# Smaller first pieces of x and of the weights, and nine warm-up matmuls fewer, in a fused conditional FFN kernel

## The chip, the cores and the metric

The kernel runs on one core of a Trainium2 chip. The metric is the device time of one execution in microseconds (us), from runs on the chip. A core has five engines that work side by side: TensorE (matmul; the profile calls it PE, and its weight loads PEld), VectorE (DVE), ScalarE (ACT), GpSimd (POOL) and SyncE (SP, which here only issues DMAs). DMAs are issued from a queue of SP, of ACT or of POOL, and all share 16 DMA engines.

## The reference

All data are float32; there are 64 x 64 tokens of 1024 features, and each batch entry has one of 16 conditions.

```python
W = weights[condition]                              # (64, 64, 64)
y = jnp.einsum('bct,bcd->bdt', x, W)                # mixes the 64 rows of one batch entry
gate_logits = jnp.einsum('bsd,ed->bse', y, gate_w)  # 8 experts
w, selected = jax.lax.top_k(gate_logits, 2)
w = jax.nn.softmax(w, axis=2)
result = jnp.einsum('bsd,od->bso', y, base_w) + base_b
w_full = sum of one_hot(selected) * w
low = jnp.einsum('bsd,erd->ebsr', y, lora_A)        # rank 16
result = result + 2.0 * jnp.einsum('ebsr,eor,bse->bso', low, lora_B, w_full)
out = x + result
```

## The kernel before, in words

The 4096 tokens are 32 tiles of 128. The condition's product mixes tokens and the other products mix features, so the kernel takes the features first: z = x times one wide matrix made of lora_A, gate_w and base_w (1160 columns, padded and cut into three column blocks of 388, of which the first uses 384), and then mixes the rows of z with a block-diagonal matrix of the tile's conditions, which GpSimd gathers. Top-2 gate, softmax and the LoRA product follow for each tile, and the sum with x and the bias is stored.

Each float32 product is made of three TensorE matmuls: an operand is split into a rounded part (xh, wh: a cast, `copy`, L234) and a remainder (xl, wl: a subtraction on VectorE, `sub`, L231), and the matmuls are wh by xh, wl by xh, wh by xl (`zstep`, L407 to L417, recorded at L414). Features come in four chunks of 256 (k), each of two halves of 128 (f). A weight block is called b*kn* or w*kn*: chunk k (1 to 4), column block n (1 to 3). The first four tiles are multiplied plainly (list PLAIN, L539): for tiles 1 and 2 the order is chunk by chunk, in it column blocks 1 and 2, in them tile 1 and then 2, so the first matmuls are those of w11 with tile 1, w11 with tile 2, w12 with tile 1, w12 with tile 2, then w21 and so on. Column block 3 follows when all chunks are there. From the fifth tile on, pairs of tiles go through a scheme with fewer products of summed operands; sums of weight blocks are prepared early on VectorE (`mix_w`, L338).

Loads at the start: `load_x` (L274) brings one chunk of one tile, 128 KB, on SP's queue; `load_w` (L313) brings a block of 388 KB on SP's queue, but w11 and w12 come as two halves (f) of 194 KB, those of w11 on ScalarE's queue. `split_x` (L280) and `split_w` (L328) cast and subtract; in the first chunk VectorE casts x and w is split half by half.

NWARM = 39 matmuls of a zero tile (L224, L225) run on TensorE before the first data are there. ScalarE loads its activation table in the same time (L324).

The order on each engine is not written by hand: `Program.add` (L88) records every step with engine, estimated cost, buffers read and written, and a due time; `Program.run` (L111) plays a list schedule with these costs and emits the instructions engine by engine. A step depends on the last writer of a buffer's key, so a smaller key lets a step start on part of a tile. Eight semaphores serve the DMAs of the SP and ACT queues in turn, so that such a DMA waits for the landing of the one that stood eight places before it.

Of the kernel before, what the change touches and what calls it, by code (L numbers as in the profile page):

```python
# [20 lines left out]
P = 128  # L21
# [10 lines left out]
W = 388  # L32
N0 = NG + T - 2 * W
CN = (N0, W, W)
OUTS = ((NG, N0, 0), (0, W, N0 - NG), (0, W, N0 - NG + W))
KQ = 4
NPAIR = NT // 2
NPLAIN = 2
TOP = 3.0e38
NWARM = 39  # L40

PE, ACT, DVE, POOL, SP = "PE", "ACT", "DVE", "POOL", "SP"

# [36 lines left out]
class Program:  # L80
# [7 lines left out]
    def add(self, engine, cost, fn, reads=(), writes=(), due=None, first=False, size=0.0, early=None, port=False,  # L88
            after=0.0):

        n = len(self.steps)
        engine, cost = (e if isinstance(e, (list, tuple)) else [e] for e in (engine, cost))
        deps = set()
        for b in list(reads) + list(writes):
            if b in self.writer:
                deps.add(self.writer[b])
        for b in writes:
            deps.update(self.readers.get(b, ()))  # L100
        for b in reads:
            self.readers.setdefault(b, []).append(n)
        for b in writes:
            self.writer[b], self.readers[b] = n, []
        deps.discard(n)
        self.steps.append(dict(eng=dict(zip(engine, cost)), fn=fn, deps=deps, first=first, size=size, port=port,
                               lag=FLIGHT + QUEUE + size * DMA if size else 0.0, after=after,
                               due=self.horizon if due is None else due,
                               early=SP in engine and not reads if early is None else early))
# [59 lines left out]
def cond_ffn_kernel(ctx, tc, xT, x, idx, cw, wall, bias, lb, out):  # L169
# [103 lines left out]

    def load_x(i, k, u):  # L274

        add(SP, ISSUE, lambda e: nc.sync.dma_start(
            xr[:, u].rearrange("p (k n) -> p k n", k=2), xT[i][:, 2 * k:2 * k + 2]), writes=[("xr", u)],
            size=8.0 * P * P)

    def split_x(us, hi=ACT):  # L280

        n = len(us)
        js = xas.two() if n == 2 else [xas.one()]
        add(hi, 0.1 + (0.115 if hi == ACT else 0.09) * 2 * n, lambda e: copy(e, some(xh, js), some(xr, us)),
            [("xr", u) for u in us], [("xh", j) for j in js])
        add(DVE, tt_cost(2 * P * n), lambda e: sub(e, some(xl, js), some(xr, us), some(xh, js)),
            [("xr", u) for u in us] + [("xh", j) for j in js], [("xl", j) for j in js], port=True)
        return js

    def sum_x(os, xs, ys, f):  # L290

        add(DVE, tt_cost(2 * P * len(os)), lambda e: nc.vector.tensor_tensor(some(xr, os), some(xr, xs), some(xr, ys), f),  # L292
            [("xr", u) for u in set(xs + ys) - set(os)], [("xr", u) for u in os], port=True)


    class Block:


        def __init__(self, name, dt=F32):
            self.name, self.dt, self.slot, self.t = name, dt, slots.one(), None  # L300
            self.keys = [("w", self.slot, f) for f in range(2)]

        def ap(self):
            if self.t is None:
# [8 lines left out]
    def load_w(m):  # L313
# [3 lines left out]
        if k == 0 and n < 2:  # L317

            for f in range(2):
                q, dma = (SP, nc.sync.dma_start) if n else (ACT, nc.scalar.dma_start)  # L320
                add(q, ISSUE, lambda e, f=f, dma=dma: dma(b.ap()[:, f:f + 1], wall[k][n][:, f:f + 1]),
                    writes=b.keys[f:f + 1], size=4.0 * P * W, early=False)
            if not n:
                add(ACT, 1.5, lambda e: nc.scalar.activation(warm, warm, AF.Exp))  # L324
            return
# [2 lines left out]
    def split_w(m, p, step=2):  # L328

        b, h, l = raw[m], Block(f"wh_{m}_{p}", F32R), Block(f"wl_{m}_{p}", F32R)  # L330
        hi[p], lo[p] = h, l
        for j in range(0, 2, step):
            a = slice(j, j + step)
            add(ACT, 0.2 + 0.00083 * W * step, lambda e, a=a: copy(e, h.ap()[:, a], b.ap()[:, a]), b.keys[a], h.keys[a])
# [69 lines left out]
    def mm_cost(n):  # L404
        return max(COL * n + SET, LEAST)

    def zstep(key, b, j, p, f, start, stop, cols=W):  # L407


        z, n = bank[b][:, :cols], slice(f * P, (f + 1) * P)  # L410

        def do(e):
            for q, (l, w) in enumerate(((xh, h), (xh, g), (xl, h))):
                nc.tensor.matmul(z, l[:, j, n], w.ap()[:, f, :cols], start=(start and q == 0), stop=(stop and q == 2),  # L414
                                 skip_group_check=True)
        h, g = hi[p], lo[p]
        add(PE, 3 * mm_cost(cols), do, [("xh", j), ("xl", j), h.keys[f], g.keys[f]], [b, "order"], due=due[key])  # L417

    def split_z(n, src, key):

# [1 line left out]
        h, l = zh[q][:, :n], zl[q][:, :n]  # L422
        add(ACT, 0.2 + 0.00085 * n, lambda e: copy(e, h, src()), [key], [("zh", q)])
        add(DVE, 0.09 + 0.00104 * n, lambda e: sub(e, l, src(), h), [key, ("zh", q)], [("zl", q)],
            port=isinstance(key, tuple))
        return q

    def outs(c):
# [152 lines left out]

    for k in range(KQ):
        for i in range(2):
            load_split_x(i, k, hi=DVE if k == 0 else ACT)
            load_split_w(f"b{k + 1}{i + 1}", step=1 if k == 0 else 2)

    chan = sb.tile([P, 1], F32, name="chan")
# [24 lines left out]
    def plain(i, c, k):  # L612
# [8 lines left out]
            if c == 0 and i > 1:  # L621
                load_cond(i)
        ks, m = LASTK if c == 2 and i < 2 else range(KQ), f"b{k + 1}{c + 1}"
        for f in range(2):
            zstep(("plain", i, c, k, f), zb[i, c], xa0[i, k], SINGLE.get(m, m), f, k == ks[0] and f == 0,
                  k == ks[-1] and f == 1, CN[c])
        left[i, k] -= 1
        if not left[i, k]:
            xas.give(xa0[i, k])
# [234 lines left out]
```

## Time and profile before

| | |
|---|---|
| median of 3 runs | 460.17 us (460.08 to 460.25) |
| the profiled execution's own time | 460.46 us |
| its span, first to last instruction | 458.7 us |
| first warm-up matmul | 1.06 us |
| first matmul on data (L414) | 5.02 us |
| first matmul with w12 | 8.10 us |
| first matmul with w21 | 10.23 us |
| DMA in the first 11.5 us / the next 11.5 us | 279 / 352 GB/s |

The page gives busy time, and the chain of work that ended last, followed back from the last instruction. The timeline lists instructions by start; in brackets stands how long the engine was idle before one, and what ended that. Busy matmuls overlap: one of 384 columns takes 0.34 us from start to end, and the next starts 0.175 us after it. SP issued the first loads at these times:

| issue, us | load | landed after, us |
|---|---|---|
| 0.74 | x, tile 1, chunk 1 (SP) | 3.4 |
| 0.74 | w11, f = 0 (ScalarE's queue) | 3.6 |
| 1.18 | x, tile 2, chunk 1 (SP) | 3.8 |
| 1.18 | w11, f = 1 (ScalarE's queue) | 4.1 |
| 1.65, 2.12 | w12, f = 0 and 1 (SP) | 4.2, 4.3 |
| 2.60 | w21 (SP) | 5.5 |
| 3.07 | x, tile 1, chunk 2 (SP) | 5.4 |
| 4.40 | w22 (SP) | 5.0 |

### The profile page before, as it was taken

How to read it: one execution, taken by the hardware profiler on the slowest of the kernel's cores; microseconds unless marked ns; L12 is line 12 of the kernel's file. 1: busy time of each engine (PE TensorE's matmuls, PEld its weight loads, DVE VectorE, ACT ScalarE, POOL GpSimd, SP SyncE). 2: the span in 40 equal slices, each digit the busy share in tenths (PEclk: the TensorE clock that was granted, in tenths of full speed). 3: DMA queues.
4: the chain of work that ended last, by engine and by line, in shares of the span. 5: the costliest groups of instructions: out<-in, count | busy, mean ns of one | idle time of the engine just before them, and what ended most of it. 6: DMA issues, size and time to landing. Idle time of an engine off the chain costs nothing.

```text
span 458.7 us, 7577 instructions
## 1 busy us (share of the span) xinstructions
PE 452.7 (99%) x2621; PEld 449.7 (98%) x2621; DVE 383.5 (84%) x941; ACT 227.2 (50%) x520; POOL 89.6 (20%) x107
## 2 busy tenths in 40 slices
PE   8999999999999999999999999999999999999995
PEld 8999999999999999999999999999999999999995
DVE  5999997879989788796987979789797988888674
ACT  5864666543736345373543646354454544546331
POOL 3030214121303021220303003030210403103000
PEclk9999999999999999999999999999999999999999
DMA  8932748977768462764847456565565746556142
GB/s 279 352 117 47 153 107 198 213 211 202 180 206 202 172 161 87 217 131 163 199 127 202 108 182 148 172 162 133 191 123 185 173 129 193 116 174 149 51 134 91
DMA packets 36229, 75.00 MB, mean 164 GB/s; under 512 B 4432, under 2 KB 22240, under 8 KB 36192
## 3 DMA queue, kind: packets, MB, share of 16 engines
q0 software_dynamic: 10560, 36.72, 33.5%
q1 hardware_dynamic: 25200, 37.32, 25.9%
q10 hardware_dynamic: 432, 0.49, 0.4%
q8 instruction: 20, 0.33, 0.3%
q14 instruction: 17, 0.14, 0.1%
HBM read 57.74 MB, written 16.78 MB: 162 GB/s over the span
## 4 chain that ended last, share of the span: by engine, by line
PE 97%; DMA 1%; DVE 1%; ACT 0%; issue 0%
PE ps_z L414 76%; PE ps_o L447 15%; PE ps_a L447 6%; DMA w_b<-in_w 1%; PE ps_a L500 1%; DVE wl_b_b L231 0%; DVE xtok L457 0%; DVE st L740 0%; ACT wh_b_b L234 0%; DVE xl L231 0%; PE ps_z L447 0%; DVE xh L234 0%
## 5 line engine op out<-in xcount | busy, mean ns | idle before, releaser
L231 DVE TENSOR_TENSOR xl<-xr,xh 128x512 fp32r<-128x512 f32 (+1 forms) x138 | 92.1, 670 | 20.0 <-ACT xh L234 19.8
L414 PE MATMUL ps_z<-wh_t_p,xh 128*128 128x388 f32 (+1 forms) x308 | 105.3, 342 | 0.1
L414 PE MATMUL ps_z<-wh_t_p,xl 128*128 128x388 f32 (+1 forms) x308 | 104.3, 339 | 0.0
L414 PE MATMUL ps_z<-wl_t_p,xh 128*128 128x388 f32 (+1 forms) x308 | 104.3, 339 | 0.0
L234 ACT CAST xh<-xr 128x512 fp32r<-128x512 f32 (+1 forms) x136 | 82.5, 610 | 37.2 <-PE ps_z L414 32.5
L740 DVE TENSOR_TENSOR st<-ps_z,st 128x388 f32<-128x388 f32 x126 | 70.2, 558 | 21.2 <-PE ps_z L414 20.2
L292 DVE TENSOR_TENSOR xr<-xr 128x256 f32<-128x256 f32 (+1 forms) x139 | 69.6, 526 | 3.6 <-DMA xr<-in_xT 3.4
L414 PE MATMUL ps_z<-wh_b_p,xh 128*128 128x388 f32 (+1 forms) x180 | 61.4, 341 | 0.0
L414 PE MATMUL ps_z<-wh_b_p,xl 128*128 128x388 f32 (+1 forms) x180 | 60.9, 338 | 0.0
L414 PE MATMUL ps_z<-wl_b_p,xh 128*128 128x388 f32 (+1 forms) x180 | 60.8, 338 | 0.0
L414 PEld LDWEIGHTS ps_z<-wh_t_p,xh 128*128 128x128 f32 x308 | 57.8, 188 | 1.2 <-DVE st L740 0.7
L414 PEld LDWEIGHTS ps_z<-wl_t_p,xh 128*128 128x128 f32 x308 | 57.9, 188 | 0.0
L414 PEld LDWEIGHTS ps_z<-wh_t_p,xl 128*128 128x128 f32 x308 | 57.9, 188 | 0.0
L464 POOL DMA_DIRECT2D out<-xtok x30 | 16.8, 560 | 193.6 <-DVE xtok L457 89.6
L234 ACT CAST zh<-st 128x388 fp32r<-128x388 f32 (+1 forms) x70 | 36.1, 517 | 22.1 <-DVE st L740 15.2
L381 POOL DMA_DIRECT2D xtok<-in_bias x28 | 27.0, 964 | 96.9 <-DMA xtok<-in_x 89.6
L394 POOL DMA_INDIRECT bdr<-in_cw,rows x32 | 36.9, 1155 | 26.4 <-DVE zl L231 17.7
L457 DVE TENSOR_TENSOR xtok<-ps_o,xtok 128x388 f32<-128x388 f32 (+1 forms) x56 | 30.9, 554 | 11.2 <-PE ps_o L447 10.7
L723 ACT ACTIVATE ps_z<-ps_z 128x388 f32<-128x388 f32 x42 | 20.1, 478 | 40.5 <-PE ps_z L414 39.4
L231 DVE TENSOR_TENSOR zl<-st,zh 128x388 fp32r<-128x388 f32 (+1 forms) x70 | 38.7, 554 | 0.9 <-ACT zh L234 0.6
L414 PEld LDWEIGHTS ps_z<-wh_b_p,xh 128*128 128x128 f32 x180 | 33.8, 188 | 0.2
L414 PEld LDWEIGHTS ps_z<-wl_b_p,xh 128*128 128x128 f32 x180 | 33.8, 188 | 0.0
(143 smaller groups left out, 873.0 us busy)
## 6 DMA issues: line engine op xcount, KB each, us to landing
xr<-in_xT SPq DMA_DIRECT2D x128, 128.0 KB, 3.2
xtok<-in_bias POOLq DMA_DIRECT2D x32, 512.0 KB, 7.1
out<-xtok POOLq DMA_DIRECT2D x30, 512.0 KB, 3.2
xtok<-in_x SPq DMA_DIRECT2D x28, 512.0 KB, 3.6
w_b<-in_w SPq DMA_DIRECT2D x10, 388.0 KB, 5.9
xtok<-in_x POOLq DMA_DIRECT2D x4, 512.0 KB, 6.6
out<-xtok SPq DMA_DIRECT2D x3, 194.0 KB, 2.2
bdr<-in_cw,rows POOLq DMA_INDIRECT x32, 5.3
```

The lines of the kernel that those rows point to most:

```text
L231: eng[e].tensor_tensor(o, a, b.bitcast(F32), ALU.subtract)
L234: (nc.scalar.copy if e == ACT else nc.vector.tensor_copy)(o, a)
L292: add(DVE, tt_cost(2 * P * len(os)), lambda e: nc.vector.tensor_tensor(some(xr, os), some(xr, xs), some(xr, ys), f), [("xr", u) for u in s ...
L381: add(POOL, 1.1, lambda e: nc.gpsimd.dma_start(xtok[j], bias.broadcast_to([P, T]), accum_op=ALU.add), writes=keys, size=TWICE * 4.0 * T * P)
L394: add(POOL, 1.04, lambda e: nc.gpsimd.indirect_dma_start(out=bdr[j], out_offset=None, in_=cw, in_offset=bass.IndirectOffsetOnAxis(ap=rows[ ...
L414: nc.tensor.matmul(z, l[:, j, n], w.ap()[:, f, :cols], start=(start and q == 0), stop=(stop and q == 2), skip_group_check=True)
L447: nc.tensor.matmul(d, l, r, start=(start and m == 0), stop=(stop and m == len(mms) - 1), skip_group_check=True)
L457: add(DVE, 0.09 + 0.00104 * (s.stop - s.start), lambda e: nc.vector.tensor_tensor(xtok[j][:, o], bank[b][:, s], xtok[j][:, o], ALU.add), [ ...
L464: add(POOL, 1.0, lambda e: nc.gpsimd.dma_start(out[i * P:(i + 1) * P, o], xtok[j][:, o]), src, size=4.0 * P * (o.stop - o.start))
L500: add(PE, 0.107, lambda e: nc.tensor.matmul(tp, low[i % 2][:, :ER], ident, is_transpose=True, start=False, stop=False, skip_group_check=True),
L723: add(ACT, 0.2 + 0.00085 * W, lambda e: nc.scalar.mul(z[b], z[x], scale), [BANKS[x]], [BANKS[b]])
L740: add(DVE, 0.09 + 0.00104 * W, lambda e: nc.vector.tensor_tensor(unit(u), a(), b(), f), reads, [ukey(u)])
```

## The change

- The first chunk of tile 1 is loaded as two DMAs of 64 KB, one for each half f, both with a due time that puts them first on SP's queue, and VectorE casts and subtracts each half by itself.
- The half f = 0 of w11 is loaded as two DMAs of 194 columns on ScalarE's queue, and cast and subtracted by columns; the half f = 1 is now one DMA on SP's queue, behind x.
- The first matmuls, of w11's f = 0 with tile 1, run as two sets of three with 194 columns instead of one with 384 (the last four columns are padding).
- NWARM goes from 39 to 30.
- Keys of x and of the weights become finer, so that the halves can be waited for one by one; w keys may be nested lists, which `add` flattens.

```diff
+HALVES = (slice(0, 194), slice(194, W))
...
-NWARM = 39
+NWARM = 30
...
+        reads, writes = ([k for q in ks for k in (q if isinstance(q, list) else [q])] for ks in (reads, writes))
...
     def load_x(i, k, u):
-        add(SP, ISSUE, lambda e: nc.sync.dma_start(
-            xr[:, u].rearrange("p (k n) -> p k n", k=2), xT[i][:, 2 * k:2 * k + 2]), writes=[("xr", u)],
-            size=8.0 * P * P)
+        for a, n in ((0, 1), (1, 1)) if (i, k) == (0, 0) else ((0, 2),):
+            add(SP, ISSUE, lambda e, a=a, n=n: nc.sync.dma_start(
+                xr[:, u, a * P:(a + n) * P].rearrange("p (k n) -> p k n", k=n),
+                xT[i][:, 2 * k + a:2 * k + a + n]), writes=xkeys("xr", [u])[a:a + n], size=4.0 * n * P * P,
+                due=a - 100.0 if n == 1 else None)
+
+    def xkeys(t, us):
+        return [(t, u, f) for u in us for f in range(2)]
...
-    def split_x(us, hi=ACT):
+    def split_x(us, hi=ACT, parts=False):
...
+        if parts:
+            for f in range(2):
+                c, k, x, y, z = slice(f * P, (f + 1) * P), 0.1 + 0.09, ("xr", us[0], f), ("xh", js[0], f), ("xl", js[0], f)
+                add(hi, k, lambda e, c=c: copy(e, xh[:, js[0], c], xr[:, us[0], c]), [x], [y])
+                add(DVE, tt_cost(P), lambda e, c=c: sub(e, xl[:, js[0], c], xr[:, us[0], c], xh[:, js[0], c]),
+                    [x, y], [z], port=True)
+            return js
...
-            self.keys = [("w", self.slot, f) for f in range(2)]
+            self.keys = [[("w", self.slot, f, h) for h in range(2)] for f in range(2)]
...
             for f in range(2):
-                q, dma = (SP, nc.sync.dma_start) if n else (ACT, nc.scalar.dma_start)
-                add(q, ISSUE, lambda e, f=f, dma=dma: dma(b.ap()[:, f:f + 1], wall[k][n][:, f:f + 1]),
-                    writes=b.keys[f:f + 1], size=4.0 * P * W, early=False)
+                q, dma = (SP, nc.sync.dma_start) if n or f else (ACT, nc.scalar.dma_start)
+                for h in range(2) if (n, f) == (0, 0) else (None,):
+                    c = HALVES[h] if h is not None else slice(0, W)
+                    add(q, ISSUE, lambda e, f=f, c=c, dma=dma: dma(b.ap()[:, f, c], wall[k][n][:, f, c]),
+                        writes=[b.keys[f] if h is None else b.keys[f][h]], size=4.0 * P * (c.stop - c.start),
+                        early=False)
...
+        if m == "b11":
+            for f, c, k in ((0, HALVES[0], 0), (0, HALVES[1], 1), (1, slice(0, W), None)):
+                x, y, z = (t.keys[f] if k is None else t.keys[f][k] for t in (b, h, l))
+                n = c.stop - c.start
+                add(ACT, 0.2 + 0.00083 * n, lambda e, f=f, c=c: copy(e, h.ap()[:, f, c], b.ap()[:, f, c]), [x], [y])
+                add(DVE, tt_cost(n), lambda e, f=f, c=c: sub(e, l.ap()[:, f, c], b.ap()[:, f, c], h.ap()[:, f, c]),
+                    [x, y], [z], port=True)
+            return
...
-    def zstep(key, b, j, p, f, start, stop, cols=W):
-        z, n = bank[b][:, :cols], slice(f * P, (f + 1) * P)
+    def zstep(key, b, j, p, f, start, stop, cols=W, half=None):
+        cols = slice(0, cols) if half is None else HALVES[half]
+        z, n = bank[b][:, cols], slice(f * P, (f + 1) * P)
...
-            load_split_x(i, k, hi=DVE if k == 0 else ACT)
+            load_split_x(i, k, hi=DVE if k == 0 else ACT, parts=(i, k) == (0, 0))
...
-        for f in range(2):
-            zstep(("plain", i, c, k, f), zb[i, c], xa0[i, k], SINGLE.get(m, m), f, k == ks[0] and f == 0,
-                  k == ks[-1] and f == 1, CN[c])
+        order = ((0, 0), (0, 1), (1, None)) if (m, i) == ("b11", 0) else ((0, None), (1, None))
+        for n, (f, h) in enumerate(order):
+            zstep(("plain", i, c, k, f), zb[i, c], xa0[i, k], SINGLE.get(m, m), f, k == ks[0] and not n,
+                  k == ks[-1] and f == 1, CN[c], h)
```

## The prediction

> **What bounds the kernel now.** I read the page first, for the engine that carries the end, then the chain that ended last for where that engine did not yet run, then the timeline of the first 16 us and the stretch around 27 us for what it waited for.
>
> ```profile
> span 458.7 us, 7577 instructions
> ...
> PE 452.7 (99%) x2621; PEld 449.7 (98%) x2621; DVE 383.5 (84%) x941; ACT 227.2 (50%) x520; POOL 89.6 (20%) x107
> ...
> PE 97%; DMA 1%; DVE 1%; ACT 0%; issue 0%
> ```
>
> TensorE carries 97% of the chain. A change that leaves its work alone can only win what TensorE idles at the start, or lose there. The chain in order of time (start, length, what) shows that start:
>
> ```profile
> 0.74 3.64 DMA w_b<-in_w
> ...
> 4.40 0.52 ACT wh_b_b L234
> ...
> 6.05 0.49 DVE wl_b_b L231
> ...
> 6.59 19.83 PE ps_z L414 x110
> ```
>
> So the first 6.59 us are: the first piece of w11 lands at 4.38, its cast, its remainder, x's remainder, and from 6.59 matmuls. The timeline (start, length, engine, line, operation, idle before it and what ended it):
>
> ```profile
> 5.00 0.19 PEld L414 LDWEIGHTS ps_z<-wh_b_b,xh 128*128 128x128 f32 x1
> 5.57 0.19 PEld L414 LDWEIGHTS ps_z<-wl_b_b,xh 128*128 128x128 f32 x1 [0.38 <-DVE wl_b_b L231]
> 6.59 0.19 PEld L414 LDWEIGHTS ps_z<-wl_b_b,xh 128*128 128x128 f32 x1 [0.39 <-DVE wl_b_b L231]
> 8.17 0.84 ACT L234 CAST wh_b_b<-w_b 128x776 fp32r<-128x776 f32 x1 [1.25 <-DMA w_b<-in_w]
> 9.04 0.97 DVE L231 TENSOR_TENSOR wl_b_b<-w_b,wh_b_b 128x776 fp32r<-128x776 f32 x1 [1.11 <-ACT wh_b_b L234]
> 11.22 0.42 DVE L231 TENSOR_TENSOR xl<-xr,xh 128x256 fp32r<-128x256 f32 x1
> 11.69 0.19 PEld L414 LDWEIGHTS ps_z<-wh_b_b,xl 128*128 128x128 f32 x1 [0.22 <-DVE xl L231]
> ```
>
> Two things are to be seen. TensorE loses 0.38 + 0.39 us in the first block, as expected. But it waits again at 11.69, for the x remainder of the second chunk's second tile, and that wait is not TensorE's doing: VectorE runs without a gap from 9.04 to the end of that operation (0.97 + 0.42 + 0.97 + 0.42 with small overlaps, 2.60 us), and it starts at 9.04 because w21 landed just before 8.17. **The second stretch hangs on w21's landing, not on when TensorE began.** VectorE then stays busy without a gap until 28.4, where this line stands in front of TensorE:
>
> ```profile
> 25.91 0.95 DVE L231 TENSOR_TENSOR wl_b_b<-w_b,wh_b_b 128x776 fp32r<-128x776 f32 x1
> ```
>
> TensorE's weight load that reads it starts at 26.91, and the matmul after it comes 0.06 us later than the 0.175 us pitch would have it. The cast that this line needs ends at 25.61 (it began at 24.77, after 1.30 us of ScalarE waiting for that block's DMA). So VectorE's line could come at most about 0.3 us sooner unless that DMA comes sooner too. After 27 us no wait over 0.1 us for data stands before 440 us.
>
> **The change part by part.** The program order of the changed kernel as built differs only at the start: the same matmuls, fewer warm-up ones, three more real ones; VectorE three more operations; all queues otherwise in the same order (one 128-column cast of bdr goes one place earlier, into ScalarE time that waits for DMA anyway).
>
> *Warm-up, 39 to 30.* The 39 run from 1.06 to 5.00, 0.101 us each; most have a weight load of 147 ns (the least is 98), so most run on a slow clock and the last few on the full one, with a slow pitch near 0.107. Thirty end at 1.06 + 30 x 0.101 to 0.107 = 4.1 to 4.25.
>
> *First piece of w11, 194 of 388 columns.* The whole piece landed at 4.38. Its half cannot come later; it saves 97 KB at the some 380 GB/s of 3.5 to 5 us, 0.26 us, and, if the x ahead of it shrinks alike, 0.5 us: 3.85 to 4.1, I take 3.95. The cast was 0.51 us at 388 columns and 0.29 at 128: 0.35 at 194, done at 4.3. First real matmul 4.3 instead of 5.02. The remainder (0.56 at 388 columns, 0.27 at 128: 0.34) gives the second at 4.65; the second half follows by about 0.45, its three matmuls done near 5.3.
>
> *Second half of w11 (f = 1), now third on SP's queue instead of second on ScalarE's.* Issue at about 1.65 instead of 1.2, but with only 194 KB of x and halves less in front of it in sum: landing between 4.8 and 5.3 (before: about 5.3), I take 5.05. Cast to 5.56, remainder to 6.1, then its last matmuls and the six of the second tile at 0.175: w12's first matmul at 7.5 to 7.6, where it stood at 8.10. **Gain so far: 0.5 us (0.2 to 0.8).** The six matmuls of 194 columns for three of 384 cost some 0.05 us and lie in the waits.
>
> *VectorE's three more operations.* 2 x 0.27 for 0.42, 2 x 0.34 for 0.56, two casts of 128 columns for one of 0.29: together 0.3 us more, ahead of 9.04. What hides it is the idle 1.11 us before 9.04; without that cover it would be 0.3 us on the path at 11.69.
>
> *SP's queue.* Two more issues at 0.45 us stand before w21, and in the built program every DMA from the ninth on waits for the landing of the one eight before it. w21 was the seventh and went at 2.60 without a wait. Now it is the ninth and waits for the first half of w11: issue at about 4.0. Behind it x21 goes at 4.4 (3.07), w22 at 4.85 (4.40), x22 at 5.3 (4.77); the later ones follow alike, and who waits for them are ScalarE's casts and through them VectorE. Does that delay w21's landing? Issued at 2.60 it landed 5.5 us later, near 8.1, behind 1032 KB. A block of the same size issued at 21.18 landed 3.5 us after its issue. From 4.0 that is 7.5, so the bytes in front decide, not the issue, and they are the same 1032 KB. Before, the stretch 7.0 to 8.0 moved only 264 GB/s where those around it moved 380: a dip of 0.3 us, whose cause the trace does not name. Bounds for w21's landing: 7.5 (no dip) to 8.6 (dip, and a gap in the stream of up to 0.5 because the issue came late). I take 7.95, between the landing of before and that landing without the dip, which is the nearest thing measured.
>
> *Smaller rows.* x11's pieces have 512 bytes per partition, w11's halves 776. The Trainium skill ("DMA: Bandwidth & Descriptors", Specifications) gives 512 B as the least size at line rate; by it these pieces cost nothing. The trace has nothing smaller than 1024 B rows for x to weigh that against; a loss of a fifth on 322 KB would be about 0.15 us at the start and is inside the bounds.
>
> *Sum.* TensorE comes to w21 0.5 us sooner, at 9.7 instead of 10.23. VectorE's run begins 0.15 us sooner. The wait at 11.69 becomes 0.22 + 0.5 - 0.15, about 0.55 us, so 0.35 of the 0.5 goes back, and 0.15 is kept. At 26.91 the same 0.15 shift of VectorE's run lets it stand. The profiled execution took 460.46 us (458.7 of span and 1.8 around it), and would be 460.3; the median of the three runs, 460.17, is 0.29 lower, and I count from that: **460.0 us.**
>
> **The clock, a rule that speaks against it.** Thirty warm-up matmuls are 3.1 us of activity. In the trace the slow weight loads (147 ns, against 98) go on to nearly 5 us, although the granted clock stands at 1.00 in every stretch: its rows do not show this phase. The Trainium skill ("TensorE: Matmul & The Clock Gate", What's actually happening) says that the full clock comes after about 3.4 us of sustained activity, judged in a window that runs freely. By the row, with the change of clock near 4.9 again, nothing is lost: the matmuls of 4.3 to 4.9 wait for data anyway. By the rule, gaps of 0.1 to 0.3 us between 4.1 and 5 may make that window count as idle, and the slow clock then stays for another 3.4 us, to 8.3.
>
> **Rivals.** *The slow clock stays (slower).* Place: from 5.6 to 8.3. Each matmul of 384 columns then costs 0.32 (384/128 of the 0.107 pitch) instead of 0.175: the three of f = 1 end near 6.7, the six of the second tile near 8.6, w12's twelve at 10.7 instead of 10.23, and the matmul of 11.69 comes at 12.1. It decides from the point where the idle between 4.1 and 4.9 is enough for the gate; price 0.4 us, time 460.6. For it: the gaps that my own sum puts there. Against it: TensorE is busy for over four fifths of that stretch. *The stream gaps because w21 waits for the first landing.* w21 lands at 8.6 and VectorE's run starts 0.45 later: 460.6. For it: the issue moves by 1.4 us. Against it: the 3.5 us row. *Supply comes sooner too.* No dip, w21 at 7.5, w22 likewise: VectorE's run moves by 0.6, TensorE keeps its 0.5 and the old wait of 0.22 shrinks: 459.6. For it: the dip is not caused by the change's parts. Against it: the later block at 24.77, which limits the gain to 0.3 unless the whole stream moves. *The gain of the first matmul reaches the end whole:* 459.4, only if everything behind moves alike.
>
> **How the numbers follow.** Main case (w21 about as before, 459.8 to 460.3) 0.45; supply sooner (459.4 to 459.8) 0.22; clock 0.12; stream gap 0.15; both of the last or something unseen, over 461.1, 0.06. The range 459.5 to 460.8 holds the first four but for their edges. A measurement of this kernel tells about 0.2%, 0.92 us, from no change. The first matmul can move by 0.9 us at most (5.0 to 4.1), and only with all of that kept would the kernel be faster by as much, so 0.03; slower by it needs w21 late by 0.9 or the clock slow for two windows, 0.10; the rest, 0.87, within.
>
> **What would show it.** Right: first L414 weight load near 4.3, w12's first near 7.6, ScalarE's cast of w21 starting at 7.7 to 8.3, the wait at 11.69 longer, about 0.5 us, and TensorE unbroken after it. Wrong: a cast of w21 at 8.6 or later (stream gap); matmuls at a pitch of 0.32 beyond 5.5 us (clock); no wait near 11 us (supply sooner). The prediction fails by more than its range only if a later part of the program is moved too, which the order of the built program does not show.

## The result, and the profile after

The changed kernel takes 462.31 us (median of 6 runs, 461.63 to 464.15), the kernel before 460.25 beside it (460.08 to 460.72): 1.0049 times as long, interval 1.003 to 1.0067. It is slower by 2.06 us; the forecast was 460.0, and its range ended at 460.8. The profiled execution took 464.15 us, the longest of the six, with a span of 462.4. The profile therefore shows more of the loss than the median execution had.

First the page: span and instructions, busy time of the engines, and the shares of the chain that ended last.

```profile
span 462.4 us, 7573 instructions
...
PE 455.3 (98%) x2615; PEld 452.9 (98%) x2615; DVE 384.4 (83%) x944; ACT 227.4 (49%) x521; POOL 89.5 (19%) x107
...
PE 97%; DMA 1%; DVE 1%; SPq 0%; issue 0%
```

TensorE still carries 97% of the chain, and its busy time grew by 2.6 us (452.7 before) although it has nine warm-up matmuls fewer. Work that became longer, not only idle time, is what to look for. The chain in order of time (start, length, what) begins with another load than before:

```profile
2.12 4.39 DMA xr<-in_xT
7.55 22.36 PE ps_z L444 x110
```

Before, it began with w11's first piece, and the 110 matmuls began at 6.59. Now it begins with the load of x's tile 2, issued at 2.12 and taking 4.39 us, and they begin at 7.55. The timeline (start, length, engine, line, operation, idle before it and what ended it) had these two operations of VectorE next to each other before the change, the cast of x's tile 2 and the remainder of w11's second half:

```profile
5.76 0.29 DVE L234 CAST xh<-xr 128x256 fp32r<-128x256 f32 x1
5.96 0.57 DVE L231 TENSOR_TENSOR wl_b_b<-w_b,wh_b_b 128x388 fp32r<-128x388 f32 x1
```

After it:

```profile
4.13 0.34 PEld L444 LDWEIGHTS ps_z<-wh_b_b,xh 128*128 128x128 f32 x1
4.68 0.52 ACT L237 CAST wh_b_b<-w_b 128x388 fp32r<-128x388 f32 x1 [0.24 <-DMA w_b<-in_w]
5.42 0.33 PEld L444 LDWEIGHTS ps_z<-wh_b_b,xh 128*128 128x128 f32 x1
6.53 0.29 DVE L237 CAST xh<-xr 128x256 fp32r<-128x256 f32 x1 [1.36 <-DMA xr<-in_xT]
6.94 0.56 DVE L234 TENSOR_TENSOR wl_b_b<-w_b,wh_b_b 128x388 fp32r<-128x388 f32 x1
7.04 0.51 ACT L237 CAST wh_b_b<-w_b 128x388 fp32r<-128x388 f32 x1 [1.84 <-DMA w_b<-in_w]
7.55 0.29 PEld L444 LDWEIGHTS ps_z<-wl_b_b,xh 128*128 128x128 f32 x1 [1.80 <-DVE wl_b_b L234]
7.72 0.33 PEld L444 LDWEIGHTS ps_z<-wh_b_b,xl 128*128 128x128 f32 x1
...
9.17 0.84 ACT L237 CAST wh_b_b<-w_b 128x776 fp32r<-128x776 f32 x1 [0.48 <-DMA w_b<-in_w]
...
13.19 0.33 PEld L444 LDWEIGHTS ps_z<-wl_b_b,xh 128*128 128x128 f32 x1
13.51 0.20 PEld L444 LDWEIGHTS ps_z<-wh_b_b,xl 128*128 128x128 f32 x1
13.88 0.19 PEld L444 LDWEIGHTS ps_z<-wl_b_b,xh 128*128 128x128 f32 x1
```

Four things are to be seen.

- **The start came sooner**, as intended: the first weight load on data at 4.13 instead of 5.00, and w11's second half is cast at 4.68.
- **VectorE is held.** Its cast of x's tile 2 at 6.53 (5.76 before) stands, as before the change, in program order ahead of the remainder of w11's second half, which TensorE needs next. That half was cast by 5.20, but its remainder starts only at 6.94, behind x. TensorE waits 1.80 us for it.
- **TensorE is slow up to 13.51.** From the first one on data, weight loads take about 0.33 us, and from 8.04 they follow each other every 0.32 us; then they take 0.19 us, every 0.175, as they did before from 5.00 on. The granted clock of the windows reads 1.00 in this stretch, because the trace's clock record begins only at 13.52; only the durations tell it here.
- **The other loads are late too**: the first half of w12 is cast at 7.04, w21 at 9.17 (8.17 before). Later profiles show how much w21 varies by itself: 7.1 to 8.3 where the loads come in time.

The windows (columns: stretch, its length, busy time of PE, PEld, DVE, ACT, POOL, granted clock, DMA share, GB/s) of the kernel before and of the changed one show where the loads lost their time:

```profile
4.00:5.00 1.00, 1.00 (x14) 1.00 (x12) 0.34 (x2) 0.51 (x1) 0.00 (x0) 1.00 1.06 377
5.00:6.00 1.00, 0.87 (x7) 0.47 (x4) 1.00 (x4) 0.61 (x2) 0.35 (x1) 1.00 1.07 388
```

```profile
4.00:5.00 1.00, 1.00 (x9) 1.00 (x7) 0.86 (x3) 0.67 (x2) 0.53 (x2) 1.00 1.07 149
5.00:6.00 1.00, 1.00 (x5) 0.75 (x4) 0.17 (x1) 0.20 (x1) 0.75 (x3) 1.00 0.84 213
```

Between 4 and 6 us the changed kernel moves 362 KB where the kernel before moved 765, with the DMA engines shown as nearly as busy (1.07 and 0.84 against 1.06 and 1.07): packets were under way and took longer.

The sum for this execution: the weight load that waited starts at 7.55 instead of 6.59, 0.96 later. From it to the first matmul with w21 is 6.33 us instead of 3.64, 2.69 more: some 18 steps at 0.32 instead of 0.175 are 2.6. Together 3.65 at 13.88. The old wait of 0.22 at 11.69 is gone, so some 3.4 are left at 34 us; then comes a steady drift of about 0.4 until 440 us. The execution took 3.69 us longer.

### The profile page after: what moved, and what is told of

Its sections match the earlier page's. It is cut to its first block, busy times and chain, and to the rows that moved or that the text cites. A ratio compares the mean times of both kernels' runs of the same rounds, so it can differ in the third digit from the quotient of the medians.

```text
span 462.4 us, 7573 instructions
## 1 busy us (share of the span) xinstructions
PE 455.3 (98%) x2615; PEld 452.9 (98%) x2615; DVE 384.4 (83%) x944; ACT 227.4 (49%) x521; POOL 89.5 (19%) x107
## 4 chain that ended last, share of the span: by engine, by line
PE 97%; DMA 1%; DVE 1%; SPq 0%; issue 0%
PE ps_z L444 76%; PE ps_o L479 15%; PE ps_a L479 6%; DMA xr<-in_xT 1%; PE ps_a L532 1%; DVE st L773 0%; SPq L280 0%; DVE xtok L489 0%; DVE wl_b_b L234 0%; DVE zl L234 0%; SPq L340 0%; PE ps_z L479 0%; DVE xl L234 0%; DVE xh L237 0%
## 5 line engine op out<-in xcount | busy, mean ns | idle before, releaser
L234 DVE TENSOR_TENSOR xl<-xr,xh 128x512 fp32r<-128x512 f32 (+2 forms) x139 | 92.4, 667 | 21.5 <-ACT xh L237 21.3
L444 PEld LDWEIGHTS ps_z<-wh_b_p,xl 128*128 128x128 f32 x180 | 33.9, 188 | 0.0
```

Source lines behind the costliest of these rows:

```text
L234: eng[e].tensor_tensor(o, a, b.bitcast(F32), ALU.subtract)
L444: nc.tensor.matmul(z, l[:, j, n], w.ap()[:, f, cols], start=(start and q == 0), stop=(stop and q == 2), skip_group_check=True)
```

## The experiments

Each ran beside the kernel before, whose median was 459.98 to 460.34 us; the ratios are to that. One execution of each was profiled, and times within a kernel are of that execution. In the quoted expectations letters stand for theories: A and B the ones named there, P that the small pieces or short rows stall the loads, Q that w11's second half on SP's queue does, R that x in two loads and the short warm-up each lose by themselves, S that the late issue of w21 stalls the loads, I that the index load does.

### What is it made of

**e1**: the changed kernel again, unchanged.

> The changed kernel once more, unaltered, for a second profile beside the first. The first one shows TensorE idle from 5.9 to 7.55 us, because VectorE's cast of x of tile 2 waits for its DMA until 6.53 and the remainder of w11's second half stands behind it, and matmuls at a pitch of 0.32 us from 7.55 to 13.51 us. If the lost time is that idle and the slow clock after it (theory A), this profile has both again, with 462 us or a little more; the end of the slow pitch may differ, by the stretches of 3.4 us in which the clock is judged. If it was one bad execution of the DMAs (theory B), x of tile 2 lands near 5 us here and the time is near 460.5.

463.06 us, ratio 1.0057 (1.0044 to 1.007). The profile is the same picture: x's tile 2 cast at 6.46, a gap of 1.74 us, weight loads of 0.33 until 13.4. Its six executions took 462.0 to 464.3 us, so the loss isn't a single bad execution.

**e2**: the changed kernel with the old warm-up.

```diff
-NWARM = 30
+NWARM = 39
```

> The changed kernel with 39 warm-up matmuls instead of 30, all else as changed. Theory A1 (the slow clock is the larger part of the loss: 19 matmuls at 0.32 instead of 0.175 make 2.7 us in the first profile): the full clock comes near 5 us, and the time falls to 460.2 to 460.8, although the loads are as late as before. Theory A2 (late loads are the larger part, w21 landing 1.0 us later than before the change): it stays at 461.3 or more, since w21 still lands near 9 us.

461.77 us, 1.0036 (1.0024 to 1.0048), so 1.3 us better than e1 beside it. The loads are as late (x's tile 2 at 6.56), so the gain is the clock's. The profiled execution is one of the longer ones (463.07): with 39 the full clock came before the data did, was kept to the gap, and was lost by it. TensorE idled 2.08 us; then the windows show it:

```profile
6.00:7.00 1.00, 0.00 (x0) 0.00 (x0) 0.44 (x3) 0.00 (x0) 0.72 (x1) 1.00 0.94 320
7.00:8.00 1.00, 0.42 (x1) 0.42 (x2) 1.00 (x4) 0.99 (x2) 0.98 (x1) 0.73 0.99 294
```

TensorE does nothing from 6 to 7, and the granted clock falls to 0.73 in the mean of the next microsecond; weight loads take 0.33 us until 10.6.

**e3**: the kernel before with `NWARM = 30`.

> The kernel before the change with 30 warm-up matmuls instead of 39, all else as before. A1: the gap from 4.2 to 5.0 us and the two waits of 0.4 us in the first block keep the clock slow for at least one more stretch of 3.4 us, to 8 us or later: 460.6 to 462. A2, or warm-up matmuls that matter only by their number: no change, 460.2, since nothing on TensorE was ready before 5.0 us.

460.51 us, 1.0007 (0.9999 to 1.0014), but single executions from 459.82 to 462.19. Its profile has a gap of 0.71 us before 4.88 and full clock after it. In the median nine warm-up matmuls fewer cost little here, but single executions pay; e7 below, whose loads also come in time, pays in the median.

**e4**: the changed kernel with the cast of x's tile 2 on ScalarE, so that VectorE isn't held.

```diff
-            load_split_x(i, k, hi=DVE if k == 0 else ACT, parts=(i, k) == (0, 0))
+            load_split_x(i, k, hi=DVE if (i, k) == (0, 0) else ACT, parts=(i, k) == (0, 0))
```

> The changed kernel with the cast of x of tile 2, first chunk, on ScalarE instead of VectorE, so that the remainder of w11's second half no longer stands behind that load on VectorE. Theory A (the hold on VectorE opens the gap that keeps the clock slow): TensorE goes on with w11's second half near 5.7 us, the gap shrinks to what the load itself leaves, and 0.5 to 1.5 us of the 2.06 come back (460.8 to 461.8). If the late landing alone is the cause: 462 as changed, the wait only moves to tile 2's matmuls.

461.62 us, 1.003 (1.0019 to 1.0041), and the runs lie within 0.67 us of each other (2.5 for the changed kernel). The one gap of 1.80 is now four of 0.16 to 0.61 us, and the clock is full from 4.7 on; it came in this execution before VectorE's hold could matter. The loads are late all the same (x's tile 2 cast at 6.74, w21 at 8.76). So hold and clock together are worth 1.4 us against e1.

### What makes the loads late

**e5** puts w11's second half back on ScalarE's queue in the changed kernel; **e6** puts it on SP's queue, behind x, in the kernel before. The line is e5's, and e6 has its reverse; both also set due times that keep the order of the loads.

```diff
...
-                q, dma = (SP, nc.sync.dma_start) if n or f else (ACT, nc.scalar.dma_start)
+                q, dma = (SP, nc.sync.dma_start) if n else (ACT, nc.scalar.dma_start)
...
```

> The changed kernel with w11's second half back on ScalarE's queue, behind the two 194-column pieces; all pieces and the 30 warm-up matmuls stay. In the profiles so far, the changed loads move 150 to 380 GB/s between 4 and 7 us where the loads of before move 375, x of tile 2 lands at 6.5 instead of 5.0 us and w21 at 8.5 to 9.2 instead of 8.1. Theory Q (the move to one queue does it: only SP's queue carries loads after 4 us, and x of tile 2 stands behind 194 KB more): x of tile 2 lands near 5, w21 near 8.2, and the time is 460.0 to 460.8. Theory P (the small rows, 512 and 776 bytes, do it): x of tile 2 lands after 6, the time stays above 461.5.

> The kernel before with one part of the change: w11's second half on SP's queue, behind x of tile 1, nothing in smaller pieces, 39 warm-up matmuls. Q: x of tile 2 lands after 6 us, w21 near 9, and the time is 461.2 to 462.5. P: x of tile 2 lands at 5.3 or sooner, w21 near 8.2, the time is 460.2 to 460.7.

e5: 461.96 us, 1.0035 (1.0021 to 1.0049); x's tile 2 is cast in time, at 5.38, and w21 at 8.04; now w11's second half is the late one (cast at 5.61, ScalarE having waited 1.32 us for it), and TensorE has a gap of 1.14 us. e6: 461.01 us, 1.0016 (1.0009 to 1.0022), with loads as before (x's tile 2 at 5.70, w21 at 8.33). Q falls as the only cause of late loads: in e6 the queue of w11's second half does not do it alone. It still costs 0.7 us there.

**e7**: the changed kernel with x in one load. **e8**: with w11's first half in one load, x in two. **e9**: as e7, with 39 warm-up matmuls. (Keys and due times that follow from these lines are left out.)

```diff
-        for a, n in ((0, 1), (1, 1)) if (i, k) == (0, 0) else ((0, 2),):
+        for a, n in ((0, 2),):
...
```

```diff
-                for h in range(2) if (n, f) == (0, 0) else (None,):
+                for h in (None,):
...
```

> The changed kernel with the first x load in one DMA of 128 KB again (still first on SP's queue; its cast and remainder stay in halves). P, if the 512-byte rows are what slows the loads: w21 lands near 8.2 and half or more of the 2.06 us comes back (461.2 or less). Q, or the 776-byte rows: as changed, 462 to 463.

> The changed kernel with w11's first half in one DMA of 194 KB again (casts, remainders and matmuls stay in halves of columns; x stays in two pieces). P, if the 776-byte rows slow the loads: w21 lands near 8.2, 461.2 or less. Q, or the 512-byte rows: as changed, 462 to 463; the first matmul comes at about 4.7 instead of 4.2 in either case.

> The changed kernel with x in one load and 39 warm-up matmuls: of the change the w11 pieces, the queue move and the split casts stay. Theory R (two causes, each enough to lose by itself: x in two 512-byte-row loads slows all loads of the first 8 us, as every profile with it shows 900 to 1120 KB landed at 6 us against 1163 to 1191 KB without it; and 30 warm-up matmuls leave the clock slow): with both undone no slow pitch after 6.5 us, w21 lands near 8.2, 460.2 to 460.9. If the queue move alone costs (it gave 461.01 by itself): 461.0. If neither was the cause: above 461.5.

e7: 462.32 us, 1.0042 (1.0028 to 1.0055). The loads are in time (x's tile 2 at 5.99, w21 at 8.18), the clock isn't: weight loads of 0.33 until 9.3, and with x whole the first weight load on data comes at 4.68 only, 0.51 us after the warm-up's last. e8: 462.36 us, 1.0043 (1.003 to 1.0057); x's tile 2 is late (6.31; 182 GB/s from 4 to 5 us), w21 is not (8.31). e9: 461.4 us, 1.0026 (1.0015 to 1.0037); loads in time (5.68, w21 7.87), slow only to 6.4. So 39 warm-up matmuls are worth some 0.7 us with the loads in time (e9 against e7). The pieces of x go with the late loads, those of w11 do not; and e9, with loads and clock both repaired, is still slower by 1.1 us.

**e10**: the kernel before with x's first load as two of 128 columns, rows of 512 bytes. **e11**: as two of 64 partitions, rows of 1024 bytes.

```diff
...
+                for f in range(2):
+                    nc.sync.dma_start(xr[:, u, f * P:(f + 1) * P], xT[i][:, f])
...
```

```diff
...
+                    a = slice(f * P // 2, (f + 1) * P // 2)
+                    nc.sync.dma_start(xr[a, u].rearrange("p (k n) -> p k n", k=2), xT[i][a, 2 * k:2 * k + 2])
...
```

> The kernel before with one part of the change: the first x load as two loads of 128 columns (rows of 512 bytes), cast and remainder whole. R: the loads are slow again, less than 1050 KB landed at 6 us, w21 at 8.5 or later, 461 to 462. If the pieces of x are innocent: 460.3.

> The kernel before with the first x load as two loads of 64 partitions each (rows of 1024 bytes as before), as the partner of the run with 512-byte rows: the same number of loads and the same bytes. If the short rows slow the loads: as before, 460.2 to 460.6. If one more load at the head of SP's queue does it: 461 to 462, as with the columns.

e10: 460.66 us, 1.001 (1.0003 to 1.0017). e11: 461.26 us, 1.0023 (1.0015 to 1.003). The windows, of e10 and then of e11:

```profile
4.00:5.00 1.00, 0.96 (x15) 0.75 (x12) 0.66 (x2) 0.74 (x2) 0.00 (x0) 1.00 1.10 381
5.00:6.00 1.00, 1.00 (x4) 0.48 (x3) 1.00 (x4) 0.55 (x2) 0.80 (x3) 1.00 1.15 357
```

```profile
4.00:5.00 1.00, 1.00 (x13) 1.00 (x11) 0.00 (x0) 0.59 (x2) 0.00 (x0) 1.00 0.68 158
5.00:6.00 1.00, 0.60 (x5) 0.36 (x3) 0.81 (x2) 0.00 (x0) 0.86 (x3) 1.00 0.99 301
```

With rows of 512 bytes at the head the queue moves 381 GB/s; with rows twice as long, in half the partitions, 158. P in the form "short rows" falls: they don't stall the loads by themselves.

**e12**: the changed kernel with x whole, 39 warm-up matmuls and both halves of w11 on ScalarE's queue (the edits of e5, e7 and e2 together): only the pieces of w11 are left.

> What the runs so far leave as the harmless part: w11's first half in two pieces of 194 columns, its second half behind them on ScalarE's queue, x whole, casts in halves, 39 warm-up matmuls. R: no slow loads, no slow pitch, the two waits of 0.4 us in the first block shrink, but w21's landing still sets the wait near 11.7 us: 460.0 to 460.4, at most 0.3 us better than before.

460.69 us, 1.0009 (1.0001 to 1.0018). The loads are in time (w21 at 7.98), there is no wait near 11.7 at all, and yet nothing is won: the wait moved to the line that stood at 25.91 before. This is its weight load, with "issue" where the remainder (26.45 to 27.42, behind a cast that began at 25.57 after 1.22 us of waiting for a DMA) had just ended:

```profile
27.47 0.19 PEld L444 LDWEIGHTS ps_z<-wl_b_b,xh 128*128 128x128 f32 x1 [0.69 <-issue]
```

**e14**: the kernel before with two loads of one row of 256 bytes ahead of w21 on SP's queue.

```diff
+                for j in range(2):
+                    nc.sync.dma_start(xr[:1, NXR - 1, 64 * j:64 * j + 64], xT[0][:1, 0, :64])
                 nc.sync.dma_start(b.ap(), wall[k][n])
```

> The kernel before, with two loads of one row of 256 bytes put ahead of w21 on SP's queue, so that w21 is issued at about 3.55 us instead of 2.60; bytes and order of all else are the same. Theory S (the late issue of w21 makes the loads of 4 to 7 us slow): 5 to 6 us moves about 210 GB/s instead of 380, x of tile 2 is cast at 6.3 or later, w12's cast 6.5 or later, w21's cast at 8.4 to 8.8, time 460.7 to 461.5. Rival (the split of x's first load itself makes them slow): x of tile 2 cast at 5.8, w21's cast at 8.2 to 8.4, time 460.3 to 460.6.

460.92 us, 1.0019 (1.0012 to 1.0026), 0.94 us more than the kernel before beside it. w21 went out at 4.07, later than meant. x's tile 2 (5.43) and w12 come in time, so S doesn't hold for the early loads; but 5 to 6 us moves only 260 GB/s, and w21 is cast at 8.74, 0.4 us after the latest of the other profiles with x in one load. That the later issue costs the 0.94 us is likely, not shown: the two small loads were added with it.

**e15**: the changed kernel with w12 as one load and x's tile 2 third on SP's queue, so that w21 goes out in a block of issues from 2.59 to 3.50.

```diff
-                due=a - 100.0 if n == 1 else None)
+                due=a - 100.0 if n == 1 else -90.0 if (i, k) == (1, 0) else None)
...
-        if k == 0 and n < 2:
+        if k == 0 and n < 1:
```

> The changed kernel, with w12 as one load instead of two and x of tile 2 third on SP's queue, so that w21 is SP's sixth load, issued at about 2.6 to 3.1 us instead of 3.58; x and w11 stay in pieces, 30 warm-up matmuls. Theory S: the loads come as in the kernel before (x of tile 2 cast at 5.8, w21's cast at 7.9 to 8.2), no gap of TensorE over 1 us, time 460.9 to 461.7 (what is left is the clock and the drift of 0.4). Rival (the split of x makes the loads slow): x of tile 2 cast at 6.3 or later, w21's cast at 8.4 or later, time 462 to 463.

463.18 us, 1.0069 (1.0051 to 1.0087). With w21 early there is still a late load, and 4 to 6 us moves 274 GB/s. S falls:

```profile
6.21 0.51 ACT L237 CAST wh_b_b<-w_b 128x388 fp32r<-128x388 f32 x1 [1.97 <-DMA w_b<-in_w]
...
8.38 0.84 ACT L237 CAST wh_b_b<-w_b 128x776 fp32r<-128x776 f32 x1 [0.28 <-DMA w_b<-in_w]
```

Now w11's second half, fourth on the queue, is the late one; w21 (8.38) is not. (The planner also ordered matmuls at 40 to 150 us otherwise in this kernel and in e16, with a wait for VectorE there, 1.0 us here and 2.4 us in e16; its time isn't comparable to the microsecond.)

**e17**: the changed kernel with the index load on GpSimd issued later, at 2.52 instead of 1.29. In all profiles so far the packets of this load began at 2.97 to 3.23 us where loads were late (and in e5), and at 3.56 to 4.30 where they were not.

```diff
+    for t in xtok[:2]:
+        nc.gpsimd.memset(t, 0.0)
     nc.gpsimd.dma_start(idx_sb, idx)
```

> The changed kernel, with two memsets ahead of the index load on GpSimd, so that the index load is issued about 1.7 us later; all other loads and orders are the same. In every run with late loads the packets of the index load began at 2.97 to 3.23 us and the low DMA rate began within 1 us of that; in the runs with loads in time they began at 3.56 to 4.30. Theory I (the index load in the middle of the first loads is what stalls them): its packets begin at 4 us or later, 4 to 6 us moves 350 GB/s or more instead of 145 to 213, x of tile 2 is cast at 5.8, w21's cast at 8.2, time 460.9 to 461.7. Rival (the early index packets are only a sign that the small pieces went through early): x of tile 2 cast at 6.3 or later, w21's cast at 8.4 or later, time 462 to 463.

462.59 us, 1.0041 (1.0028 to 1.0055). Its packets begin at 4.56, and the loads are late as ever:

```profile
6.20 0.29 DVE L239 CAST xh<-xr 128x256 fp32r<-128x256 f32 x1 [1.54 <-DMA xr<-in_xT]
...
8.76 0.84 ACT L239 CAST wh_b_b<-w_b 128x776 fp32r<-128x776 f32 x1 [0.51 <-DMA w_b<-in_w]
```

I falls: the early index packets were a sign, not the cause. What stalls the loads stays open, but the profiles together tell when it happens. The mean rate from 4 to 6 us, in GB/s:

| x's first load | w11's second half on ScalarE's queue | on SP's queue |
|---|---|---|
| one DMA | 382 (before), 363 (e3), 391 (e12), 386 (e13), 320 (e14) | 367 (e6), 348 (e7), 357 (e9), 344 (e18) |
| two of 128 columns | 355 (e5), 369 (e10) | 181 (changed), 240 (e1), 211 (e2), 239 (e4), 258 (e8), 274 (e15), 214 (e16), 198 (e17) |

The low rate comes with both together, in eight profiles of eight, and with neither alone (e14's 320 has its two added loads). So P and Q fall only as single causes; the change made both moves at once. Two loads of 64 partitions stall the stream without the second (230 in e11).

### The drift

The changed kernel and e1, e2, e4 to e9 and e17 lost another 0.3 to 0.5 us between 34 and 440 us, bit by bit, without a wait. (e3 lost 0.55 there in two steps, at two waits for VectorE.) The instructions there are the same in the same order; what differs is in which order the weight slots are first used, and with it where their tiles lie in SBUF: in the built programs 30 of 128 tiles have another address in the changed kernel and in each of the others with the drift, none in e10 and e11 and four in e12, which have no drift.

**e13**: the kernel before with the tiles placed as in the changed one. **e18**: e9 with the tiles placed as in the kernel before.

```diff
+    for s in [0, 3, 7, 1, 2, 10, 14, 4, 17, 5, 21, 8, 24, 9, 11, 36, 39, 42]:
+        sb.tile([P, 2, W], F32, name=f"place{s}", tag=f"w{s}")
     pr.run()
```

> The kernel before, with nothing changed but where the weight blocks' tiles lie in SBUF: they are allocated in the order in which the changed kernel first uses them. Theory A (placement makes the drift): the start is as before, and TensorE falls behind the kernel before by 0.35 to 0.5 us between 34 and 440 us, median 460.7. Rival (the drift comes from the late start or from the order of the loads, not from the placement): no drift, 460.3.

> The changed kernel with x in one load, 39 warm-up matmuls (as e9) and the SBUF placement of the kernel before; w11 stays in pieces with its second half on SP's queue. e9 took 461.4 us, 1.2 more than the kernel before; its profile fell behind that of before by 0.28 us up to 27 us and by 0.4 more between 88 and 440 us. Theory A (placement makes the drift here too): the fall behind is the same at 88 and at 440 us, median 460.8 to 461.1, ratio about 1.0017. Rival (the drift in the changed kernel comes from something else): the 0.4 us are still there, 461.3 to 461.5.

e13: 460.46 us beside 459.98, 1.0013 (1.0005 to 1.0021). e18: 460.86 us, 1.0009 (1.0001 to 1.0018), where e9 had 1.0026. The timelines give two matmuls that all kernels share, a transpose at 34 and one at 446 us; first of the kernel before, then of e13, of e9 and of e18:

```profile
33.72 0.27 PE L500 MATMUL ps_a<-ident,low 128*128 128x128 f32 x1
446.07 0.27 PE L500 MATMUL ps_a<-ident,low 128*128 128x128 f32 x1
```

```profile
33.38 0.27 PE L500 MATMUL ps_a<-ident,low 128*128 128x128 f32 x1
446.10 0.27 PE L500 MATMUL ps_a<-ident,low 128*128 128x128 f32 x1
```

```profile
34.03 0.27 PE L532 MATMUL ps_a<-ident,low 128*128 128x128 f32 x1
446.91 0.27 PE L532 MATMUL ps_a<-ident,low 128*128 128x128 f32 x1
```

```profile
34.19 0.27 PE L532 MATMUL ps_a<-ident,low 128*128 128x128 f32 x1
446.50 0.27 PE L532 MATMUL ps_a<-ident,low 128*128 128x128 f32 x1
```

Between the two lie 412.35 us before, 412.72 with the changed kernel's placement alone, 412.88 in e9, and 412.31 when e9 gets the old placement. The drift is the placement, shown in both directions and followed by every profile; by which path an address costs TensorE time stays open.

**e16**: the changed kernel with every suspect repaired (e15's loads, 39 warm-up matmuls, e4's cast, the old placement: no tile has another address).

> The changed kernel with every suspect repaired: w12 as one load and x of tile 2 ahead of w11's second half (w21 issued at about 2.6 us), 39 warm-up matmuls, the cast of x's tile 2 on ScalarE, SBUF placement of the kernel before. If the list of causes (late loads, lost clock, hold on VectorE, placement) is whole: 460.0 to 460.5, the same as before, with a wait near 11.7 to 12 us that takes back what the earlier start gave. If a cause is missing: 460.9 or more, and the profile shows where.

462.35 us, 1.0044 (1.003 to 1.0058). The repair failed: w11's second half was late (cast at 6.85), and the wait of 2.4 us came later, with the order of matmuls that e15 has too. But there is no drift after 147 us, and it shows the clock best. Its weight loads:

```profile
7.42 0.19 PEld L444 LDWEIGHTS ps_z<-wh_b_b,xh 128*128 128x128 f32 x1 [1.94 <-ACT wh_b_b L237]
8.01 0.29 PEld L444 LDWEIGHTS ps_z<-wl_b_b,xh 128*128 128x128 f32 x1 [0.41 <-DVE wl_b_b L234]
8.18 0.34 PEld L444 LDWEIGHTS ps_z<-wh_b_b,xl 128*128 128x128 f32 x1
...
10.74 0.33 PEld L444 LDWEIGHTS ps_z<-wl_b_b,xh 128*128 128x128 f32 x1
11.06 0.23 PEld L444 LDWEIGHTS ps_z<-wh_b_b,xl 128*128 128x128 f32 x1
11.29 0.19 PEld L444 LDWEIGHTS ps_z<-wh_b_b,xh 128*128 128x128 f32 x1
```

and its window, with the granted clock in the third column from the end:

```profile
8.00:10.00 2.00, 1.99 (x6) 1.99 (x7) 1.37 (x3) 1.91 (x4) 0.03 (x1) 0.50 1.04 374
```

After an idle of 1.94 us the first load still takes 0.19. At 7.73 the clock halves, and 3.41 us later, with one wait of 0.41 between, it is back.

The clock records of all the traces tell more. After its first entry, in each of them, every stretch of half or full clock up to the end of the matmuls lasts a whole number of 3.413 us: one of half clock in e2 (7.47 to 10.88), e15 (8.44 to 11.85) and e16 (7.73 to 11.15), and 131 to 133 of full clock to the end in all twenty traces. The warm-up starts at 1.06 us in all of them, but the full clock comes anywhere from 3.88 (e10) to 13.61 (e1). So here the clock is set in windows of 3.41 us which don't start with the program. Three readings follow for gaps:

- A gap can cost the clock or not. The windows in which e16, e2 and e15 lost it had TensorE busy for 0.48, 0.50 and 0.58 of the time; e5, with a gap of 1.14 us, had 0.67 and kept it, as did e8 (0.73), e4 (0.77) and e3 (0.80).
- One gap can spoil two windows. Counted back from 13.52, the changed kernel's windows meet at 6.70, inside its gap. The one before (3.28 to 6.70) was busy for 0.84 and the one after (6.70 to 10.11) for 0.75, and neither brought the full clock; the next, without idle, did. In e1 and e17 they meet at 6.79 and 6.50, inside the gap too.
- Thirty warm-up matmuls, 3.1 us, are shorter than one window, and 39, 4.0 us, are longer. With 30 it depends on where the windows fall whether the clock comes early: at 4.28 to 5.51 in e3, e4, e5 and e8, at 9.39 in e7, after 13 in the changed kernel, e1 and e17.

How busy a window has to be to win the clock isn't settled: e10 won it with 0.83, e7 did not with 0.93.

## Why the prediction was wrong

The parts stand in one line of ratios: the changed kernel 1.0049 and 1.0057 (e1), with 39 warm-up matmuls 1.0036 (e2), with x in one load as well 1.0026 (e9), with the old placement as well 1.0009 (e18). In that order that is 0.6 to 1.0 us for the shorter warm-up, 0.5 for the late loads with what they do to the clock, 0.8 for the placement (0.4 to 0.6 by the profiles), and 0.4 left, which e18's profile has in two waits of 0.6 us, at 6.75 and 27.38, for remainders on VectorE. The intervals reach about half a microsecond to each side; they tell the order of sizes.

- *First matmul* (forecast 4.3): right, 4.20, behind the last warm-up matmul; its cast had begun at 3.59. *Second half* (forecast landed at 5.05): its cast began at 4.68, better than forecast.
- *w12's first matmul at 7.5 to 7.6*: wrong, 10.28. **The step that failed first is the one that let w11's second half go on "to 6.1" after its cast.** Its remainder ended at 7.50. The step counted VectorE's three more operations as 0.3 us of work and left out their order: the cast of x's tile 2 stands ahead of that remainder, and waits for a load. The prediction named whom a wait of SP holds, not whom this one holds.
- *"the bytes in front decide, not the issue, and they are the same 1032 KB"*: wrong. The same bytes took longer: 149 and 213 GB/s where 377 and 388 were counted on. The bounds for w21 (7.5 to 8.6) were drawn from the old stream with its one dip, and nothing was set aside for x's tile 2 and w12, whose landing was not forecast at all. The sum weighed the two moves, x in two loads and w11's second half on SP's queue, one by one; by the table above it is their pair that stalls the stream. e14 makes it likely that a late issue counts too.
- *The slow clock*: the rival had the mechanism and the sign, and its place and size were wrong. It was priced at one more window, 5.6 to 8.3, 0.4 us, with a chance of 0.12. In the profiled execution the clock was slow to 13.5, at a cost of 2.7 us; in the medians the nine warm-up matmuls cost 0.6 to 1.0. The idle was expected between 4.1 and 4.9, where TensorE was in fact busy throughout; the gap that counted came at 6 us, from the late load, and lay across two windows. The Trainium skill ("TensorE: Matmul & The Clock Gate", What's actually happening) has both halves, sustained activity and windows that run freely; e16's row (slow for 3.41 us, then full) agrees with it. The error was to price the rule by its shortest case, with the loads taken to be in time.
- *"only if a later part of the program is moved too, which the order of the built program does not show"*: the later part was slower with the order unchanged. Order is not placement; the addresses of the built program would have shown the move.
- *Short rows*: right to give them nothing (e10).
- *The wait at 11.69 grows and takes the gain back*: right as a mechanism where the loads are in time: e9 waits 0.37 us at 11.86, and e12, which has no wait there, meets the line of 25.91 instead.

The forecast let only 0.15 us of the gain at the first matmul reach the end, and even that is more than any run showed: e12, the part of the change without losses at the start, is 0.35 us slower than the kernel before beside it. No kernel tried beats the kernel before.

## What to carry to other kernels

Before moving the start of a kernel, list for each engine the instruction behind every one that waits for a DMA: a cast that isn't urgent, queued ahead of one that is, turns any late load into idle TensorE. Keep the warm-up longer than one clock window (3.41 us here) and let it run into the first data, since a gap can be paid twice, once as idle time and again as whole windows at half speed. Try two moves of loads together as well as apart, since here only the pair slowed the stream; and an edit that changes the order in which tiles are first used also moves their addresses, so compare addresses before reading a difference of a tenth of a per cent.

## What the hardware showed that was not expected

- SBUF placement alone changed the pace of the same matmuls by 0.09% (412.35 to 412.72 us), and by 0.14% in the pair e9 and e18.
- With the same bytes queued, the mean DMA rate between 4 and 6 us was 344 to 391 GB/s or 181 to 274, by small changes in the first few loads: x in two loads of columns lowered it only together with w11's second half on SP's queue (two loads of 64 partitions alone gave 230, two tiny loads added 320). The cause is not found.
- The clock changed only at the ends of windows of 3.413 us, whose place differed from execution to execution; full clock was lost in windows with TensorE busy for 0.58 of the time or less and kept with 0.67 or more.
- A kernel whose start has a gap spreads: the six executions of the changed kernel lie between 461.6 and 464.2, the six of the kernel before beside them between 460.1 and 460.7. With the gap broken up (e4) they lie within 0.67 us again. The clock windows, which fall differently in each execution, fit that; only one execution of each kernel has a trace.
